# Ten gathered tiles instead of eight beside an attention, and one graph's product moved between the scoring matmuls

## The chip, the cores and the metric

The kernel runs on one core of one Trainium2 chip. The metric is the device time of one execution in microseconds (us), the median of several runs. A profile is one further execution, recorded instruction by instruction.

## The reference

Input x is 64 graphs of 256 nodes with 256 features; adj is one sparse symmetric 256x256 weight matrix, the same for every graph. Four layers follow each other: three "scoring" layers (L0, L1, L3) and an attention layer (L2) between the second and the third of them. Cut to what matters, with the batch index left out:

```
scoring layer:
  pre_u = h @ W1[:256];  pre_v = h @ W1[256:]
  S[u,v] = sigmoid(relu(pre_u[u] + pre_v[v] + b1) . W2 + b2)
  a = (S * adj)^T @ h                    # only pairs (u,v) with an edge matter
  m = (adj @ h) * h                      # called "mixed" in the kernel
  h = beta1*h + beta2*(a @ Wa + ba) + beta3*(m @ Wm + bm)
attention layer:
  f = h @ W1^T;  f1 = f . W2 + b2
  h = softmax(leaky_relu(f1[i] + f1[j]) + adj) @ f + bias2 + h
```

## The kernel before, in words

**Tiling.** Since S is multiplied by adj, a score is needed only for node pairs with an edge. The kernel numbers the edges on the chip (`edges`, once) and sorts them into 16 blocks of up to 128 pairs, each given by a triple (k, m, i); the diagonal (`own`) and up to 64 pairs that don't fit (`left`) are kept apart. One block of two graphs is a tile of 128 pairs x (2 graphs x 256 features). Its sum pre_u[u] + pre_v[v] is made in one of two ways:

- The eight blocks in FAST are *made* on the tensor engine: ScalarE copies rows of pu and pv into `pre` (`rows_u`, `rows_v`, lines 754 and 763), and a matmul with the 0/1 matrix `pick` (L700) puts the 128x512 sums into PSUM pool `ga`, which has three buffers.
- The eight blocks in FETCHED are *fetched*: pu and pv are written to tables in DRAM (L633, SP queue), and the GpSimd queue issues two indirect DMAs per tile (L745, `fetch`): one gathers the rows of u, the second gathers those of v and adds them. The list FETCHES sets their order, 18 issues a stage with the two for `left`; `issue_after` keeps them in that order. The first six (AHEAD) are issued as soon as the first half of the tables is written, the others when the stage begins that scores this pair.

Either way VectorE then does two operations per tile (`rated`, L664), one a graph: relu, times w2row, summed into a column of `raw`. ScalarE turns columns into scores by a tanh (`rated_all`, L684): first the EARLY columns (the blocks with m = 0, the diagonal and `left`), then the LATE ones (m = 1). From these VectorE makes `rm` (L692).

**Staging.** Graphs are taken in pairs, in two streams "a" and "b" of 16 pairs each. While one pair is being scored (the *heavy* side: `scores`, with its iterators `made`, `got` and `end`), the other goes through everything else (the *light* side): `after` (`spread` puts the scores back into `sa`, L790 and L792; `finish` makes the layer's output, L281 with `sa`, L369 or L355), the attention, and `before` (the products with W1, L628, copies to pu and pv, L629 and L630, the table writes, and at its end `mixed`, L281 with `adj`). One such pairing is a stage, one call of `beside`. Six stages make a round, and there are 16 rounds, 96 stages:

| stage | scored (heavy) | beside it (light) |
|---|---|---|
| 1 | a, L0 | b: after L3, before L0 of the next pair |
| 2 | b, L0 | a: after L0, before L1 |
| 3 | a, L1 | b: after L0, before L1 |
| 4 | b, L1 | a: after L1, attention, before L3 |
| 5 | a, L3 | b: after L1, attention, before L3 |
| 6 | b, L3 | a: after L3, before L0 of the next pair |

So `mixed` of the pair that stage 4 scores is done at the end of stage 3, and that of stage 5 at the end of stage 4. In what follows a stage is taken to begin at the LATE tanh of the stage before.

**What sets the order.** Each engine runs its own queue in the order in which a scheduler put it when the program was built. The source steers it by hand: every `yield` of the light side says how many tiles of `made` and of `got` are to be placed there (`yield 0, 1`: none made, one fetched), and `beside` advances both iterators by that. `early` (L774 and L778: the `left` pairs and the diagonal go into `sa`) follows the sixth fetched tile. At the end of `before` stands `yield REST_OF_IT`, which places all tiles that are left, and then comes `mixed`, whose matmuls run on the tensor engine while the last scores, their tanh and `rm` are made. The multiplication of `mixed` by hT on VectorE (L795) is kept back in the list `later` until `spread` has been done.

**Buffers.** The first four fetched tiles (FIRST) have a buffer for each stream; the other four share one buffer. PSUM has five buffers `ps` and three `ga`.

Of the kernel before, what the change touches and what calls it, by code (L numbers as in the profile page):

```python
# [9 lines left out]
FP = mybir.dt.float32  # L10
# [5 lines left out]
P = 128  # L16
# [16 lines left out]
FAST = [(0, 0, 2), (0, 0, 3)] + [(0, 1, i) for i in range(4)] + [(1, 0, 2), (1, 0, 3)]  # L33
FETCHED = [(k, 0, i) for k in range(2) for i in (0, 1)] + [(1, 1, i) for i in range(4)]
FIRST = 4

FETCHES = [(0, 0), (1, 0), (2, 0), (0, 1), (3, 0), (1, 1)]
FETCHES += [(-1, 0), (2, 1), (4, 0), (3, 1), (5, 0), (-1, 1), (6, 0), (4, 1), (7, 0), (5, 1), (6, 1), (7, 1)]

AHEAD = 6  # L40

# [16 lines left out]
def quarter(q):  # L58
    return slice(q * 64, (q + 1) * 64)

# [18 lines left out]
def adj_seq_kernel(ctx: ExitStack, tc: tile.TileContext, a: dict, out: bass.AP):  # L79
# [15 lines left out]
    mm = nc.tensor.matmul  # L95
# [36 lines left out]
    def z_weights(l):  # L132
        for kept, n, beta in ((wm, "Wm", "beta3"), (wa, "Wa", "beta2")):
            kept[l] = const.tile([P, 2, D], FP, name=l + n)
            nc.sync.dma_start(out=kept[l], in_=a[l + n].rearrange("(c p) e -> p c e", p=P))
            nc.scalar.mul(kept[l], kept[l], sca(l + beta))
        zbias[l] = const.tile([P, 2], FP, name=l + "zbias")
        zb = const.tile([P, 2], FP, name=l + "zb")
        nc.vector.tensor_scalar(zb, vecs[:, VEC[l + "ba"], :], sca(l + "beta2"), None, ALU.mult)
        nc.vector.scalar_tensor_tensor(  # L140
# [5 lines left out]
    for l in GNN:  # L146
        halfb2[l] = const.tile([P, 1], FP, name=l + "halfb2")
        nc.vector.tensor_scalar(halfb2[l], sca(l + "b2"), 0.5, None, ALU.mult)
    twob2 = const.tile([P, 1], FP, name="twob2")
    nc.vector.tensor_scalar(twob2, sca("L2_gnn_b2"), 2.0, None, ALU.mult)  # L150
# [7 lines left out]
    def counts(keep, pool, pc):  # L158
# [3 lines left out]
        nc.vector.tensor_scalar(mask, adj, 0.0, None, ALU.not_equal)  # L162
# [6 lines left out]
        nc.vector.tensor_tensor_scan(upto.rearrange("p s v -> p (s v)"), flat, flat, 0.0, ALU.add, ALU.bypass)  # L169
        past = pool.tile([P, 8], FP, name="past")  # L170
        nc.vector.memset(past, 0.0)
        nc.vector.tensor_copy(past[:, 1:8], upto[:, 0:7, 63])
        deg = pool.tile([P, 8], FP, name="deg")
        nc.vector.tensor_tensor(deg, upto[:, :, 63], past, ALU.subtract)
# [17 lines left out]
        nc.vector.tensor_copy(first, t[:, 0:8])  # L192
        last = keep.tile([P, 8], FP, name="last")
        nc.vector.tensor_tensor(last, first, deg, ALU.add)

        over = pool.tile([P, 8], FP, name="over")
        nc.vector.tensor_scalar(over, t[:, 8:16], -128.0, 0.0, ALU.add, ALU.max)
        begin = keep.tile([P, 9], FP, name="begin")
        nc.vector.memset(begin, 0.0)
        nc.vector.tensor_tensor_scan(begin[:, 1:9], over, over, 0.0, ALU.add, ALU.bypass)  # L200
        t = pc()
        mm(out=t[:, 0:1], lhsT=other, rhs=begin[:, 8:9], start=True, stop=True)
        nc.vector.tensor_scalar(begin, begin, t[:, 0:1], None, ALU.add)
        number = keep.tile([P, 8, 64], FP, name="number")
        shift = pool.tile([P, 8], FP, name="shift")
        nc.vector.tensor_tensor(shift, first, past, ALU.subtract)
        nc.vector.tensor_tensor(number, upto, shift.unsqueeze(2).to_broadcast([P, 8, 64]), ALU.add)
        nc.vector.tensor_tensor(number, number, mask.rearrange("p m (s v) -> p (m s) v", v=64), ALU.mult)
# [3 lines left out]
    with tc.tile_pool(name="pc", bufs=2, space=bass.MemoryType.PSUM) as pc, tc.tile_pool(name="cnt", bufs=1) as cnt:  # L212
# [3 lines left out]
        nc.vector.tensor_scalar(many, end, float(LEFT), None, ALU.is_gt)  # L216
# [11 lines left out]
    def attention_weights(one, psum):  # L228
# [8 lines left out]
        nc.vector.tensor_copy(w2q[:, :, D], t[:, 0:2])  # L237
        for c in range(2):
            nc.vector.tensor_scalar(qb[:, c, :], ones, w2q[:, c, D : D + 1], None, ALU.mult)

    def last_bias(one):
# [3 lines left out]
        nc.vector.tensor_scalar(zbrow, zbrow, sca(LAST + "beta2"), None, ALU.mult)  # L245
        nc.vector.scalar_tensor_tensor(zbrow, bmrow, sca(LAST + "beta3"), zbrow, ALU.mult, ALU.add)
# [19 lines left out]
    def stages(pools):  # L266
# [16 lines left out]
        def flip(o, src):  # L283

            for m in range(2):
                for c in range(2):
                    nc.tensor.transpose(o[:, m, blk(c)], src[:, c, blk(m)], ident)  # L287
# [22 lines left out]
        def mixed(st, l, later=None):  # L310

            st["mT"] = mT = one.tile([P, 2, 2, N], FP, tag="mT" + st["side"], name="mT")
            for g in range(2):
                t = psum()
                product(t, st["h"][g], adj)
                times = (mT[:, :, g, :], t, st["hT"][:, :, g, :], ALU.mult)
                if later is None:
                    nc.vector.tensor_tensor(*times)
# [647 lines left out]
```

## Time and profile before

| what | value |
|---|---|
| median of 3 runs | 3519.05 us (3515.6 to 3520.39) |
| the profiled execution's own time | 3512.57 us |
| its span, first to last instruction | 3510.1 us |
| granted TensorE clock | 0.993 |
| busy: PE matmul / PE weight load | 3447.8 us (98%) / 2108.7 us (60%) |
| busy: VectorE / ScalarE / GpSimd | 2610.0 us (74%) / 1598.8 us (46%) / 2230.7 us (64%) |
| DMA: moved, mean rate | 587.25 MB, 167 GB/s |
| queue 0 (the fetches): bytes, share of 16 engines | 427.93 MB, 61.4% |

The page lists PE (matmul), PEld (weight load, overlaps PE), DVE (VectorE), ACT (ScalarE), POOL (GpSimd) and SP (the queue that issues plain DMAs). A row of a timeline has the start in us, the time from the first start to the last end, engine, line, operation, out<-in, the shape, and how many instructions were merged; in brackets the idle time of the engine before it and what ended it. Ends of matmuls are modelled and consecutive matmuls overlap, so the distance between starts tells more than a length. A product of fp32 operands shows as two matmul records, so one made tile is two L700 records (1536 in 96 stages of eight tiles).

Over stages 2 to 95 of the trace, measured from LATE tanh to LATE tanh, the medians of the six stages are 31.1, 32.6, 32.3, 40.0, 42.6 and 35.2 us.

### The profile page before, as it was taken

Reading aid. Unit: us, or ns where it says so; the run is one execution under the profiler, and the core shown is the slowest. Engines: PE = TensorE matmul, PEld = TensorE weight load, DVE = VectorE, ACT = ScalarE, POOL = GpSimd, SP = SyncE. Lnnn points to the kernel's source line nnn. Section 1 sums busy time; section 2 is a strip of 40 time slices with the busy share of each in tenths; the row PEclk is TensorE's granted clock in tenths of the full one; section 3 lists DMA queues with packets and bytes.
Section 4 is the critical chain, followed back from the end, with each engine's and each line's share of the span. In section 5 each row is a group of like instructions: output and inputs, shape, how many; then the busy total and the mean of one; then the engine's idle time right before and its main releaser. Section 6 shows DMA issues by size and latency. Waiting matters only on the chain.

```text
span 3510.1 us, 48385 instructions
## 1 busy us (share of the span) xinstructions
PE 3447.8 (98%) x14328; PEld 2108.7 (60%) x14328; DVE 2610.0 (74%) x10584; ACT 1598.8 (46%) x2929; POOL 2230.7 (64%) x1754
## 2 busy tenths in 40 slices
PE   6999999999999999999999999999999999999998
PEld 3566565656656566565666656656565665656655
DVE  5778686777777777777777777768677777777776
ACT  2454444444444444544444444444444444445452
POOL 3757667575666757667576675766757566675764
PEclk7999999999999999999999999999999999999999
DMA  5768777686777868778687786877768687786865
GB/s 149 168 151 189 155 184 165 163 180 153 186 156 174 177 143 193 158 175 182 142 195 158 181 170 155 188 155 185 163 165 178 149 188 154 179 181 148 192 148 114
DMA packets 274733, 587.25 MB, mean 167 GB/s; under 512 B 37024, under 2 KB 54304, under 8 KB 274464
## 3 DMA queue, kind: packets, MB, share of 16 engines
q0 software_dynamic: 190464, 427.93, 61.4%
q1 hardware_dynamic: 82416, 154.96, 12.6%
q8 instruction: 116, 1.90, 0.2%
q10 hardware_dynamic: 1584, 1.20, 0.1%
q14 instruction: 153, 1.25, 0.1%
HBM read 466.51 MB, written 117.44 MB: 166 GB/s over the span
## 4 chain that ended last, share of the span: by engine, by line
PE 67%; DVE 4%; POOL 3%; DMA 3%; issue 2%; ACT 0%; POOLq 0%; DVEq 0%
PE ps L281 13%; PE ga L700 13%; PE ps L628 12%; PE ps L369 8%; PE ps L355 5%; PE ps L790 4%; PE ps L451 3%; PE ps L410 3%; POOL fetched L745 2%; PE ps L287 2%; DMA fetched<-tablev,ids_v 2%; PE ps L774 2%; DVE junk L664 2%; PE ps L404 1%; DVE rm L692 1%
## 5 line engine op out<-in xcount | busy, mean ns | idle before, releaser
L745 POOL DMA_INDIRECT fetched<-tablev,ids_v x768 | 1211.3, 1577 | 351.0 <-issue 237.4
L745 POOL DMA_INDIRECT fetched<-tableu,ids_u x768 | 766.8, 998 | 806.1 <-DMA tableu<-pu 576.1
L700 PE MATMUL ga<-pre,pick 128*128 128x512 f32 x1536 | 775.2, 604 | 10.5 <-DVE junk L664 7.9
L628 PE MATMUL ps<-L_gnn_w,hT 128*128 128x512 f32 x1536 | 695.4, 596 | 5.7 <-DMA hT<-in_xT_dram 5.7
L664 DVE SCALAR_TENSOR_TENSOR junk<-ga,L_gnn_w2row 128x256 f32<-128x256 f32 x1536 | 583.5, 420 | 119.8 <-PE ga L700 114.8
L664 DVE SCALAR_TENSOR_TENSOR junk<-fetched,L_gnn_w2row 128x256 f32<-128x256 f32 x1536 | 596.1, 419 | 32.6 <-DMA fetched<-tablev,ids_v 32.1
L763 ACT COPY pre<-pv 64x512 f32<-64x512 f32 x768 | 473.4, 616 | 107.1 <-DVE pv L630 76.3
L628 PEld LDWEIGHTS ps<-L_gnn_w,hT 128*128 128x128 f32 x1536 | 285.1, 191 | 334.6 <-issue 311.2
L754 ACT COPY pre<-pu 64x1024 f32<-64x1024 f32 x384 | 392.9, 1039 | 3.8
L700 PEld LDWEIGHTS ga<-pre,pick 128*128 128x128 f32 x1536 | 274.9, 191 | 163.6 <-issue 111.9
L372 DVE TENSOR_TENSOR hT<-hb,ps 128x512 f32<-128x512 f32 x128 | 88.0, 688 | 379.0 <-PE ps L369 379.0
L281 PE MATMUL ps<-adj,h 128*128 128x256 f32 x1536 | 361.0, 387 | 6.6 <-DVE own L639 4.7
L281 PE MATMUL ps<-sa,h 128*128 128x256 f32 x1536 | 363.7, 382 | 3.0 <-DVE sa L792 2.6
L281 PEld LDWEIGHTS ps<-sa,h 128*128 128x128 f32 x1536 | 288.9, 190 | 119.3 <-issue 47.3
L629 ACT COPY pu<-ps 128x256 f32<-128x256 f32 x384 | 142.2, 370 | 467.6 <-PE ps L628 449.1
L281 PEld LDWEIGHTS ps<-adj,h 128*128 128x128 f32 x1536 | 284.0, 190 | 77.0 <-issue 34.3
L692 DVE TENSOR_TENSOR rm<-gva,val 128x256 f32<-128x256 f32 x768 | 277.4, 420 | 37.9 <-ACT val L685 27.7
L333 ACT ACTIVATE hb<-hT,L_gnn_zbias,scas 128x512 f32<-128x512 f32 x128 | 97.4, 807 | 450.4 <-DVE hT L372 363.7
L790 PEld LDWEIGHTS ps<-rm,gu 128*64 128x64 f32 x3072 | 175.0, 137 | 123.1 <-PE ps L281 59.1
L369 PE MATMUL ps<-mT,L_gnn_Wm 128*128 128x512 f32 x512 | 240.6, 592 | 0.0
L369 PE MATMUL ps<-aT,L_gnn_Wa 128*128 128x512 f32 x512 | 240.6, 592 | 0.0
L790 PE MATMUL ps<-rm,gu 128*64 128x128 f32 x3072 | 218.5, 280 | 14.6 <-DVE rm L692 12.4
(156 smaller groups left out, 4074.3 us busy)
## 6 DMA issues: line engine op xcount, KB each, us to landing
tableu<-pu SPq DMA_DIRECT2D x192, 256.0 KB
tablev<-pv SPq DMA_DIRECT2D x192, 256.0 KB
hT<-in_xT_dram SPq DMA_DIRECT2D x32, 512.0 KB
h<-in_x_dram SPq DMA_DIRECT2D x64, 256.0 KB
out_dram<-h SPq DMA_DIRECT2D x64, 256.0 KB
fetched<-tableu,ids_u POOLq DMA_INDIRECT x768
fetched<-tablev,ids_v POOLq DMA_INDIRECT x768
L_gnn_w<-in_L_gnn_W_dram SPq DMA_DIRECT2D x6, 256.0 KB
```

What stands on the lines that cost most here:

```text
L281: mm(out=o[:, m, :], lhsT=lhs[:, c, blk(m)], rhs=rhs[:, c, :], start=c == 0, stop=c == 1)
L355: mm(out=z[:, m, :], lhsT=y[:, c, g, blk(m)], rhs=w[:, c, :], start=j == 0 and c == 0, stop=j == 1 and c == 1)
L369: mm(out=z, lhsT=w[:, c, blk(m)], rhs=y[:, c], start=j == 0 and c == 0, stop=j == 1 and c == 1)
L628: mm(out=t, lhsT=hT[:, c, g, blk(m)], rhs=w1[l][:, c], start=c == 0, stop=c == 1)
L629: nc.scalar.copy(pu[:, m, g, :], t[:, 0, :])
L664: nc.vector.scalar_tensor_tensor(junk, t, 0.0, w2row[l], ALU.max, ALU.mult, accum_out=raw[:, i : i + 1])
L692: nc.vector.tensor_tensor(rm[:, k, ms, g, :], gva[:, k, ms, :], val[:, i : i + 4].unsqueeze(2).to_broadcast([P, 4, 64]), ALU.mult)
L700: mm(out=t, lhsT=pick[:, k, 4 * m + i, :], rhs=pre[:, n], start=True, stop=True)
L745: this = nc.gpsimd.indirect_dma_start(out=to, out_offset=None, in_=rows, in_offset=bass.IndirectOffsetOnAxis(ap=ids, axis=0), compute_op=( ...
L754: nc.scalar.copy(st["pre"][h, f : f + n], st["pu"][h, m].rearrange("p g d -> p (g d)").unsqueeze(1).to_broadcast([64, n, 2 * D]),)
L763: nc.scalar.copy(st["pre"][halves[1 - k], n], st["pv"][halves[i % 2], i // 2].rearrange("p g d -> p (g d)"))
L790: mm(out=t[h, :, quarter(i)], lhsT=gu[:, k, 4 * m + i, :], rhs=rm[:, k, 4 * m + i], start=True, stop=True)
```

## The change

- **Beside an attention** (stages 4 and 5; `more` names the pairs: b at L1, a at L3) the last two tiles of FAST, (0,1,2) and (0,1,3), are fetched too: ten fetched, six made. Their four indirect DMAs stand among the last of FETCHES_MORE, 22 issues instead of 18. The shared buffer of the later fetched tiles grows from four to six tiles.
- **Half of mixed as a filling.** In these two stages `before` does `mixed` for graph 0 only; graph 1's four products are put into `made` behind its third tile, write to a `ga` buffer, and are multiplied by hT at once.
- **Order of tiles.** FAST now begins with the four blocks of m = 0, so the EARLY tanh needs four made tiles rather than all, and the placing lists are new (STEPS for `finish`, `beside` in `before`).
- **Where the light side is "after L0, before L1"** (stages 2 and 3, `placed`), the made tiles, the fetched tiles' scores, the diagonal's and the tanh are tied behind the last instruction issued on their engine (`behind`, with a recording wrapper `Noting` around the engines), and `early` comes before the fifth fetched tile.
- **The diagonal of L1** is made from pu and pv in SBUF by one 128x512 addition per half, in `scores`, rather than by two 128x256 additions that read PSUM in `before`.

Through `Noting`, nearly every compute instruction of the changed kernel is recorded under one line of that wrapper, L79. The core of the diff:

```diff
-FAST = [(0, 0, 2), (0, 0, 3)] + [(0, 1, i) for i in range(4)] + [(1, 0, 2), (1, 0, 3)]
+FAST = [(k, 0, i) for k in range(2) for i in (2, 3)] + [(0, 1, i) for i in range(4)]
+MORE = FAST[6:]
-FETCHES += [(-1, 0), (2, 1), (4, 0), (3, 1), (5, 0), (-1, 1), (6, 0), (4, 1), (7, 0), (5, 1), (6, 1), (7, 1)]
+FETCHES += [(-1, 0), (2, 1), (4, 0), (3, 1), (-1, 1), (5, 0), (6, 0), (4, 1), (7, 0), (5, 1), (6, 1), (7, 1)]
+FETCHES_MORE = FETCHES[:-2] + [(8, 0), (6, 1), (9, 0), (7, 1), (8, 1), (9, 1)]
+STEPS = {
+    GNN[0]: [(1, 1), (1, 1), (0, 1), (1, 0), (0, 1), (2, 1)],
+    GNN[1]: [0, 0, 0, (0, 1), (0, 1), 1],
+    LAST: [1, 1, (0, 1), (1, 1), (0, 1), (2, 1)],
+}
...
-        def mixed(st, l, later=None):
+        def mixed(st, l, later=None, graphs=(0, 1), buffers=None):
...
+                t = buffers.tile([P, 2, 256], FP, tag="ga", name="ga") if buffers else psum()
...
+        def more(st, l):
+            return (st["side"], l) in (("a", LAST), ("b", GNN[1]))
...
-            got = {LAST: (1, 0, 1, 1), GNN[1]: (1, 1, 1, 1), GNN[0]: (0, 0, 2, 1)}[l]
+            beside = {LAST: [0, (0, 1), (0, 1), (0, 1)], GNN[1]: [0] + [(0, 1)] * 3, GNN[0]: [0, 0, (0, 2), (0, 1)]}[l]
...
-            yield from mixed(st, l, later if past else None)
+            yield from mixed(st, l, later if past else None, (0,) if more(st, l) else (0, 1))
...
+            blocks, fast = (FETCHED + MORE, FAST[:6]) if more(st, l) else (FETCHED, FAST)
+            t = one.tile([P, len(FETCHED + MORE) - FIRST, 2, D], FP, tag="fetched", name="fetched")
...
             def made():
-                for n, (k, m, i) in enumerate(FAST):
+                for n, (k, m, i) in enumerate(fast):
                     t = ga.tile([P, 2, D], FP, tag="ga", name="ga")
-                    mm(out=t, lhsT=pick[:, k, 4 * m + i, :], rhs=pre[:, n], start=True, stop=True)
+                    with stay(tensor):
+                        mm(out=t, lhsT=pick[:, k, 4 * m + i, :], rhs=pre[:, n], start=True, stop=True)
...
+                    if n == 2 and more(st, l):
+                        yield from mixed(st, l, None, (1,), ga)
...
-                        for _ in made:
-                            yield
-                        rated(left, REST)
+                        if placed:
+                            while len(count) < 4:
+                                next(made)
+                        else:
+                            for _ in made:
+                                yield
+                        with stay(vector):
+                            rated(left, REST)
                         rated_all(EARLY, 0)
                         yield
+                        if placed:
+                            early(st)
+                            yield
...
-                    if f == FIRST + 1:
+                    if f == FIRST + 1 and not placed:
                         early(st)
```

The order that the build gives the tensor engine between `early` of one stage and of the next, counted in matmuls of the program (two records each), shows the move. Stage 4 into 5, the part up to the first products with the scores, and the part within the attention:

```
before                                  changed
ro,guo x4  adj,h x8  pre,pick x1        ro,guo x4  gnn_w,hT x4  adj,h x4
rm,gu x16  pre,pick x1                  rm,gu x8  pre,pick x1  rm,gu x8  pre,pick x1
sa,h x8                                 sa,h x8
...
w2q,hT x8  pre,pick x3  ident,e x4      w2q,hT x8  adj,h x4 (into ga)  pre,pick x1  ident,e x4
```

## The prediction

> **What bounds the kernel now.** I read the page first: its engine shares and the group of the made tiles.
>
> ```profile
> span 3510.1 us, 48385 instructions
> PE 3447.8 (98%) x14328; PEld 2108.7 (60%) x14328; DVE 2610.0 (74%) x10584; ACT 1598.8 (46%) x2929; POOL 2230.7 (64%) x1754
> L700 PE MATMUL ga<-pre,pick 128*128 128x512 f32 x1536 | 775.2, 604 | 10.5 <-DVE junk L664 7.9
> ```
>
> PE has work from end to end. Busy alone proves little, since matmuls overlap, so I took the distances between their starts. Within a run of like records they are 0.429 us for 512 columns and 0.216 for 256. Summed at these prices, a stage of the middle rounds leaves only 0.9 to 2.1 us, 9.1 us a round of 213. Some 7.4 of that repeats at fixed places, where matmuls of other row or column groups follow each other (0.1 to 0.2 us each). True waits are about 1.7 us a round: 0.5 before stage 2 (`mixed` waits for PSUM that VectorE's `own` holds), 0.8 before stage 3 and 0.4 before stage 4 (L790 waits for `rm`). So PE's issue is the bound in each stage; taking a matmul away pays as long as nothing else comes late.
>
> Next the timeline of PE where stage 4 ends and 5 begins (tanh at 1915.77), and in the attention of stage 5:
>
> ```profile
> 1909.01 5.32 PE L628 MATMUL ps<-L_gnn_w,hT 128*128 128x512 f32 x12
> 1914.25 1.13 PE L774 MATMUL ps<-ro,guo 64*128 64x256 f32 x8
> 1915.32 3.72 PE L281 MATMUL ps<-adj,h 128*128 128x256 f32 x16
> 1918.88 1.02 PE L700 MATMUL ga<-pre,pick 128*128 128x512 f32 x2
> 1919.83 1.97 PE L790 MATMUL ps<-rm,gu 128*64 128x128 f32 x32
> 1921.72 1.12 PE L700 MATMUL ga<-pre,pick 128*128 128x512 f32 x2
> ...
> 1939.97 2.74 PE L700 MATMUL ga<-pre,pick 128*128 128x512 f32 x6
> 1942.54 0.60 PE L287 MATMUL ps<-ident,e 128*128 128x128 f32 x4
> ```
>
> No row has an idle bracket. Between the last product with W1 and L790, PE has 5.6 us of cover (1914.25 to 1919.83) for scores, tanh and `rm`; inside the attention three made tiles (2.57 us) cover the softmax.
>
> Then ScalarE and VectorE over the same boundary, which give what that cover hides:
>
> ```profile
> 1913.05 1.04 ACT L754 COPY pre<-pu 64x1024 f32<-64x1024 f32 x1
> 1914.10 1.24 ACT L763 COPY pre<-pv 64x512 f32<-64x512 f32 x2
> 1915.37 0.37 ACT L629 COPY pu<-ps 128x256 f32<-128x256 f32 x1
> ```
>
> ```profile
> 1916.84 1.25 DVE L778 SCALAR_TENSOR_TENSOR sa<-diag,val,ps 128x256 f32<-128x256 f32 x3
> 1918.01 1.42 DVE L692 TENSOR_TENSOR rm<-gva,val 128x256 f32<-128x256 f32 x4
> ```
>
> `rm` is done at 1919.43, 0.4 us before PE asks, and 1.6 us of its lateness is `early` (L778), queued ahead of it. Last the GpSimd queue, stage 5's chain of fetches:
>
> ```profile
> 1915.31 0.98 POOL L745 DMA_INDIRECT fetched<-tableu,ids_u  x1 [15.29 <-DMA tableu<-pu]
> ...
> 1919.96 1.56 POOL L745 DMA_INDIRECT fetched<-tablev,ids_v  x1 [1.16 <-DMA fetched<-tableu,ids_u]
> 1921.83 0.98 POOL L745 DMA_INDIRECT fetched<-tableu,ids_u  x1 [0.31 <-issue]
> ...
> 1942.82 1.54 POOL L745 DMA_INDIRECT fetched<-tablev,ids_v  x1 [0.30 <-issue]
> 1957.87 0.98 POOL L745 DMA_INDIRECT fetched<-tableu,ids_u  x1 [13.50 <-DMA tableu<-pu]
> ```
>
> Eighteen issues take 29 us, then GpSimd idles 13.5 us until the next tables are written. An issue costs 0.98+0.30 us (u) or 1.55+0.30 (v). The first v waits for the first u to land, 4.65 us after its issue; the trace's DMA records put the last packet of stage 5's chain 4.3 to 5.7 us (median 5.2) after the last issue began.
>
> **What the Trainium skill says.** "Perfetto Trace Analysis", Identifying the Most-Contended Engine: matmul busy time is no good measure of how near PE is to its peak. The trace agrees: the made tile's record lasts 604 ns, its starts are 429 apart; I price by starts. "TensorE: Matmul & The Clock Gate", Back-to-back issue gap: about N/2.4 + 2.5 ns, 216 for 512 columns. Here the gap is 429, twice that for each record, and a tile has two; the measured value is used. "DMA: Bandwidth & Descriptors", Anatomy of one DMA — SWDGE (gpsimd) path: about 2.0 us plus bytes/436e3, an estimate of 2.6 us for a fetch of 256 KB. The trace shows 4.65 and 5.2 with other fetches in flight; I take 5.2. "Perfetto Trace Analysis", DMA Instruction — SWDGE (GPSIMD): the profiled window is the writing of descriptors, not the movement, which fits a 1.55 us row that lands 5 us after its start.
>
> **The change, part by part.**
>
> *Two tiles less to make.* Four records of 0.429 us are 1.72 us of PE a stage; 32 stages: **-54.9 us**. With them go one L754 copy and two of L763 (2.3 us of ScalarE a stage, which at 46% gains nothing). VectorE's scoring is the same for both kinds, 419 and 420 ns: zero.
>
> *Two tiles more to fetch.* 2 x (1.28 + 1.85) = 6.3 us of GpSimd and 1 MB of DMA a stage. It lies in the idle 13.5 us (15.3 in stage 4), which shrink to 7, if the last tile lands in time. In stage 5 the chain starts, by the new order, about 5.6 us after the second product with W1 (4.6 before; the third now stands behind `early`'s matmuls). The last v is issued 33.7 us into the chain, so it lands at 5.6 + 33.7 + 5.2 = 44.5 us. The next stage's same point comes 40.8 us after (42.6 less 1.72), and VectorE asks for the tile 4.0 us past that (1.0 matmuls of `early`, 1.7 L778, 0.7 another tile, the rest pv): 44.8. Spare 0.3 us, and about 1.6 more before PE notices at L790, since `mixed` after stage 5 is whole. I take zero; the ends are -0 and +1.5 us in stage 5 (+24). Stage 4's chain starts 4.4 us before its stage, so it has some 4 us more room. Queue 0 rises from 4.46 to 5.5 MB in these stages, whose DMA share is 0.63 and 0.69 now: no limit. The first two fetched tiles are now scored inside `finish`, about 12 us into stage 5, when the second has just landed (v issued at 7.3, plus 5.2); VectorE idles some 4 us there before hT (L372), so a short wait costs nothing, one over 4 us would hold hT.
>
> *Half of mixed moved.* Its eight records (1.72 us) are neither added nor removed. In the attention they stand in for the two tiles that went: 1.72 + 0.86 = 2.58 us of filler against 2.57, so the softmax stays covered. Its multiplication by hT (0.68 us, L795 before) is queued on VectorE ahead of the second graph's maxima (L423) and holds one of three `ga` buffers meanwhile; two tiles' scores (1.4 us) that stood ahead of them are gone: nothing. At the boundaries into stages 4 and 5 they are missed, but `early` has moved ahead of the last products too. Into stage 5, from the end of `early`'s matmuls: PE 3.5 (two products with W1) + 1.7 (half of mixed) + 1.0 (first half of L790) + 1.05 (a made tile) = 7.3; VectorE and ScalarE: the ScalarE queue above (pre, pre, pu) delays the last pu to 5.0, pv 5.35, tanh and add 5.5, `rm` and one `own` 7.4, plus 0.2 to reach PE. Wait: 0.3 us. Into stage 4 the same sum gives 8.2 for PE and 9.3 + 0.2 for `rm` less one made tile, 9.15: 0.35, against 0.4 now. A `rm` that is wholly uncovered would cost 1.72 in both; a gain isn't excluded (0.4). I take +0.25 a round. The order also puts a made tile between the halves of L790 in these two stages (0.15 + 0.10 + 0.09 + 0.10 us of switching in the rows before stage 1) and takes one away before stage 2: net +0.44.
>
> *Stages 2 and 3.* `early` comes before the turn (L287) and the last products, so L778 no longer stands ahead of `rm`: from the end of its matmuls `rm` is ready at 8.8, and PE asks for its second half at about 9.8. The 0.8 before stage 3 goes. `own` of L1 no longer reads PSUM, so the 0.5 before stage 2 goes: **-1.3 us a round**. The ends are 0 (a new wait takes their place) and -1.3. Ties add no wait between engines; behind a tied instruction that waits stand the later tiles' scores and pv, for which PE has several us of other work. Bounds: -0.3 to +1 us a stage, taken zero. The L1 diagonal costs 0.69 instead of 0.84 us of VectorE a half: nothing.
>
> Sum a round: -3.43 - 1.3 + 0.25 + 0.44 = -4.0 us; over 16 rounds -65, less about a tenth for the edges, where the first rounds' waits are others: **-58 us**. The profiled execution, 3512.6 us (3510.1 of span and 2.5 around), would become 3454; it lies 6.5 us below the median, 3519.05, which becomes **3461**.
>
> **The rivals.**
> - *The cover is missed (20%).* `rm` comes later than my sum and the waits of stages 4 and 5 grow by 0.5 to 1.5 us each: 16 to 48 us back, 3477 to 3509. For it: the spare times are tenths of a us, and the outcome hangs on ScalarE's queue. Against: L778 left the way.
> - *The last fetch decides, slower (6%).* If the ninth and tenth tile land late in both attention stages, LATE tanh, `rm` and L790 wait, and each us costs 32 us. It turns slower from 1.8 us in both stages beyond what is covered; at 2.5 us the time is 3461 + 80 = 3541. For it: stage 5's spare of 0.3. Against: stage 4's spare, the 7 us that GpSimd still idles, and DMA shares well under those of stage 6 (0.89).
> - *The tiles were free fillings (3%).* If they only filled waits, removing them changes nothing: 3519. Against: no idle brackets, and the same amount of filler in the new order.
>
> **How the numbers follow.** The likeliest case, PE stays the bound (68%), covers 3440 to 3477; better than that 3%. What a measurement can tell from no change is 0.2%, 7 us. Range 3442 to 3495: it holds most of the first case and the larger part of the first rival. Faster 0.91, same 0.03, slower 0.06.
>
> **What would show it.** Made-tile records fall from 1536 to 1408, fetches rise by 128. Stages 4 and 5 become 1 to 2 us shorter, 2 and 3 about 0.5, 1 and 6 stay. GpSimd's wait for tables falls by some 200 us in all. Wrong it would be if L790's wait for `rm` grows in stages 4 and 5, if VectorE's wait for fetched tiles (32 us now) grows, or if stages 2 and 3 get longer.

## The result and the profile after

| | before | changed |
|---|---|---|
| median | 3519.72 us (3515.6 to 3520.84) | 3497.7 us (3493.48 to 3503.58) |
| ratio, with its 95% interval | | 0.9942 [0.9926, 0.9958] |
| profiled execution, and its span | 3512.57, 3510.1 us | 3499.89, 3498.2 us |
| granted clock | 0.993 | 0.993 |

The change gains 22 us. The forecast was 58 us, and 3497.7 lies just outside its range (3442 to 3495). In the two profiled executions the spans differ by 11.9 us only: that of before lies 7 us under its median, that of the changed kernel 2 us above. The page of the changed kernel, the parts that answer to those shown of before:

```profile
span 3498.2 us, 48226 instructions
PE 3391.1 (97%) x14200; PEld 2079.5 (59%) x14200; DVE 2626.2 (75%) x10526; ACT 1554.0 (44%) x2833; POOL 2409.6 (69%) x1882
...
q0 software_dynamic: 204800, 461.49, 66.6%
...
L79 PE MATMUL ga<-pre,pick 128*128 128x512 f32 x1408 | 721.5, 607 | 36.0 <-ACT pre L79 24.6
```

The counts are those of the forecast: 1408 records of made tiles for 1536, 128 issues more on GpSimd. What is new stands at the end of the last line: TensorE idled 36 us ahead of made tiles, 24.6 of them for `pre`, ScalarE's copy. Before it was 10.5, most of it for VectorE. The waits of TensorE in the whole trace (us in total, times, the longest one), first of the kernel before, then of the changed one:

```profile
PE ps L790 <- DVE rm L692: 12.4, 10, 6.0
PE ga L700 <- DVE junk L664: 7.9, 3, 6.8
...
PE ps L281 <- DVE own L639: 4.7, 5, 2.4
```

```profile
PE ps L79 <- DVE rm L79: 31.0, 33, 6.0
PE ga L79 <- ACT pre L79: 24.6, 30, 1.3
```

Summed over all its rows this view gives 57.5 us of waiting before and 102.1 after: 44.6 more. The work that went is 54.9 us by the prices of the forecast, and 54.9 less 44.6 is 10.3, near the 11.9 by which the spans differ. So the sum fits tiles that were worth what was forecast, with waits that took most of it back: 18.6 us more for `rm` and 24.6 for `pre`, for which the view of before has one wait of 0.3 us. A second pair of traces, c_before and c_after of the third series below, gives the same sum: 59.8 and 97.4 us of waits, 37.6 more, and spans that differ by 15.7 us.

From LATE tanh to LATE tanh the medians of the six stages, measured as for before, are now 31.1, 30.9, 32.5, 40.6, 42.4 and 35.1 us. Stages 4 and 5, which lost the tiles, were to become 1 to 2 us shorter; stage 4 is 0.6 longer and stage 5 only 0.1 shorter. Only stage 2 gained clearly, 1.6 us. (The half of `mixed` that moved also carries TensorE work from stage 3 to 4 and from 4 to 5, so the sum says more than one stage.)

*Where `pre` is late.* The boundary from stage 4 into stage 5 (LATE tanh at 1904.58), TensorE first, then ScalarE:

```profile
1898.37 1.13 PE L79 MATMUL ps<-ro,guo 64*128 64x256 f32 x8
1899.44 3.70 PE L79 MATMUL ps<-L_gnn_w,hT 128*128 128x512 f32 x8
1902.97 1.89 PE L79 MATMUL ps<-adj,h 128*128 128x256 f32 x8
1904.80 1.09 PE L79 MATMUL ps<-rm,gu 128*64 128x128 f32 x16
1906.90 1.12 PE L79 MATMUL ga<-pre,pick 128*128 128x512 f32 x2 [1.01 <-ACT pre L79]
```

```profile
1902.92 1.24 ACT L79 COPY pre<-pv 64x512 f32<-64x512 f32 x2
1904.19 0.37 ACT L79 COPY pu<-ps 128x256 f32<-128x256 f32 x1
1904.58 0.31 ACT L79 ACTIVATE val<-raw,L_gnn_halfb 128x16 f32<-128x16 f32 x1
1904.93 0.22 ACT L79 ACTIVATE val<-val 128x16 f32<-128x16 f32 x1
1905.17 1.04 ACT L79 COPY pre<-pu 64x1024 f32<-64x1024 f32 x1
1906.23 2.53 ACT L79 COPY pre<-pv 64x512 f32<-64x512 f32 x4
```

The made tile at 1906.90 is the new stage's first. Its last row copy is the first of the four at 1906.23 (2.53/4 = 0.63 us, so done at 1906.86). Ahead of it on ScalarE stand the copy of the last product (pu), tanh, the addition and the 1.04 us copy for tiles 2 and 3. From the start of half of `mixed` (1902.97, the last product just ended) to `pre` that is 3.9 us; TensorE has 1.83 + 1.09 us of work for it, 2.9. Before, ScalarE's queue began in the same way (last pu, tanh, addition, a 1.04 us copy, then `pre`), but between the last product and the first made tile lay `early`'s matmuls and the whole of `mixed`: 1914.25 to 1918.88, 4.6 us. At the boundary into stage 6 `mixed` is whole, and only `early` has moved away ahead of the products:

```profile
1940.64 1.13 PE L79 MATMUL ps<-ro,guo 64*128 64x256 f32 x8
1941.71 3.70 PE L79 MATMUL ps<-L_gnn_w,hT 128*128 128x512 f32 x8
1945.24 3.62 PE L79 MATMUL ps<-adj,h 128*128 128x256 f32 x16
1949.59 1.12 PE L79 MATMUL ga<-pre,pick 128*128 128x512 f32 x2 [0.72 <-ACT pre L79]
```

Over the whole trace the wait into stage 5 is there in all 16 rounds, 16.4 us in sum, and that into stage 6 in 13 of them, 7.4 us.

*Where `rm` is late.* At the start of stage 2 the second half of L790 now follows the first without a made tile between; it waits in 13 of the 16 rounds, 10.1 us in sum (0.43 us in most, 1.1 to 2.1 in four), more than the 4.7 us of the PSUM wait (`own`) that went there. At the start of stage 4 it waits 7.9 us in 11 rounds and at the start of stage 1 4.5 us in six. Each of these, and three of the four long ones at the start of stage 2, begins 2.6 to 2.9 us after a wait of VectorE for a fetched tile, and is as long as that to within about half a us (in round 11 at the start of stage 1, 1.22 us for 1.25); the plain 0.43 us of stage 2 has none ahead of it. The 5.7 us at the start of stage 3 went. VectorE's waits show the late tiles, first of the kernel before, then of the changed one:

```profile
DVE hT L372 <- PE ps L369: 379.0, 128, 4.6
...
DVE junk L664 <- DMA fetched<-tablev,ids_v: 32.1, 25, 2.9
```

```profile
DVE junk L79 <- DMA fetched<-tablev,ids_v: 203.7, 148, 3.1
...
DVE hT L79 <- PE ps L79: 100.4, 75, 2.7
```

The wait for fetched tiles rose from 32.1 to 203.7 us. Most of it (3.7 and 5.4 us a stage) is in stages 4 and 5, nearly all at the first two fetched tiles, where VectorE had waited for TensorE anyway: its waits for L369's PSUM (hT) fell from 379 to 100 us. In the last 8 us before a LATE tanh, where a late tile delays `rm`, it is 2.3 us a round in the 13 rounds of the middle, for 1.5 before.

### The profile page after: what moved, and what is told of

The parts are those of the page before. It is cut to its first block, busy times and chain, and to the rows that moved or that the text cites. A ratio compares the mean times of both kernels' runs of the same rounds, so it can differ in the third digit from the quotient of the medians.

```text
span 3498.2 us, 48226 instructions
## 1 busy us (share of the span) xinstructions
PE 3391.1 (97%) x14200; PEld 2079.5 (59%) x14200; DVE 2626.2 (75%) x10526; ACT 1554.0 (44%) x2833; POOL 2409.6 (69%) x1882
## 4 chain that ended last, share of the span: by engine, by line
PE 62%; POOL 10%; DMA 10%; DVE 8%; issue 7%; ACT 3%; another core or an unknown queue 0%; POOLq 0%; ACTq 0%; SPq 0%; DVEq 0%
PE ps L79 48%; PE ga L79 13%; POOL fetched L820 9%; DMA fetched<-tablev,ids_v 6%; DVE junk L79 3%; DMA fetched<-tableu,ids_u 3%; ACT pre L79 2%; DVE rm L79 1%; POOL left L820 1%; DVE sa L79 1%; DMA tableu<-pu 1%; DVE own L79 1%; ACT val L79 1%; ACT pu L79 1%; DVE mT L79 0%
## 5 line engine op out<-in xcount | busy, mean ns | idle before, releaser
L820 POOL DMA_INDIRECT fetched<-tablev,ids_v x832 | 1313.7, 1579 | 415.3 <-issue 256.1
L820 POOL DMA_INDIRECT fetched<-tableu,ids_u x832 | 840.5, 1010 | 548.8 <-DMA tableu<-pu 285.4
L79 DVE SCALAR_TENSOR_TENSOR junk<-fetched,L_gnn_w2row 128x256 f32<-128x256 f32 x1664 | 642.4, 418 | 205.8 <-DMA fetched<-tablev,ids_v 203.7
L79 PE MATMUL ga<-pre,pick 128*128 128x512 f32 x1408 | 721.5, 607 | 36.0 <-ACT pre L79 24.6
L79 PE MATMUL ps<-L_gnn_w,hT 128*128 128x512 f32 x1536 | 706.7, 597 | 5.8 <-DMA hT<-in_xT_dram 5.8
L79 DVE SCALAR_TENSOR_TENSOR junk<-ga,L_gnn_w2row 128x256 f32<-128x256 f32 x1408 | 537.3, 419 | 110.6 <-PE ga L79 94.6
L79 PEld LDWEIGHTS ps<-L_gnn_w,hT 128*128 128x128 f32 x1536 | 279.7, 190 | 323.2 <-issue 296.3
L79 ACT COPY pre<-pv 64x512 f32<-64x512 f32 x704 | 434.1, 617 | 70.8 <-DVE pv L79 47.3
L79 ACT COPY pre<-pu 64x1024 f32<-64x1024 f32 x352 | 361.4, 1044 | 7.4
L79 PE MATMUL ps<-sa,h 128*128 128x256 f32 x1536 | 359.8, 380 | 4.7 <-DVE sa L79 4.7
L79 PEld LDWEIGHTS ps<-sa,h 128*128 128x128 f32 x1536 | 291.7, 190 | 114.4 <-issue 62.5
L79 PEld LDWEIGHTS ga<-pre,pick 128*128 128x128 f32 x1408 | 248.5, 190 | 183.6 <-issue 92.5
L79 ACT COPY pu<-ps 128x256 f32<-128x256 f32 x384 | 142.8, 372 | 478.2 <-PE ps L79 450.3
L79 ACT ACTIVATE hb<-hT,L_gnn_zbias,scas 128x512 f32<-128x512 f32 x128 | 97.4, 807 | 479.3 <-DVE hT L79 368.1
L79 DVE TENSOR_TENSOR rm<-gva,val 128x256 f32<-128x256 f32 x768 | 279.8, 419 | 28.7 <-ACT val L79 21.2
L79 PE MATMUL ps<-adj,h 128*128 128x256 f32 x1280 | 296.8, 383 | 3.9 <-issue 3.9
L79 PEld LDWEIGHTS ps<-adj,h 128*128 128x128 f32 x1280 | 241.6, 191 | 74.1 <-issue 40.0
L79 DVE TENSOR_TENSOR pv<-ps,L_gnn_b1row 128x256 f32<-128x256 f32 x384 | 161.3, 420 | 135.5 <-ACT pu L79 128.8
L79 PEld LDWEIGHTS ps<-rm,gu 128*64 128x64 f32 x3072 | 174.7, 137 | 144.5 <-issue 54.1
L79 PE MATMUL ps<-rm,gu 128*64 128x128 f32 x3072 | 218.8, 280 | 32.6 <-DVE rm L79 31.0
L79 ACT COPY aT<-ps 128x512 f32<-128x512 f32 x192 | 112.4, 585 | 299.7 <-PE ps L79 267.5
L79 PE MATMUL ps<-mT,L_gnn_Wm 128*128 128x512 f32 x512 | 240.6, 592 | 0.0
```

Source lines behind the costliest of these rows:

```text
L79: self.last = getattr(self.engine, op)(*a, **k)
L820: this = nc.gpsimd.indirect_dma_start(out=to, out_offset=None, in_=rows, in_offset=bass.IndirectOffsetOnAxis(ap=ids, axis=0), compute_op=( ...
```

## The experiments

Two theories were to be told apart. *A:* TensorE's new waits at the starts of stages 5 and 6 are the loss; cover was moved away, and the first made tile's copy is late in ScalarE's queue. *B:* the fetches are late; VectorE, which takes its work in order, waits for a tile near a stage's end, and tanh and `rm` come late behind it. A third possibility, that the placing and the ties as such cost time, is what undoing the two named parts leaves over.

The experiments ran in four series, each on one chip with its own runs of the kernel before (medians 3520.6, 3502.6, 3514.7 and 3515.3 us); the changed kernel was run again in the last two. Compare times within a series, and ratios to before across them.

### First series: parts undone, and ScalarE's order

x_first:

```diff
                     rows_v(st, 4 - 4 * m, 2, 0)
+                    st["first"] = scalar.last.ins
...
-                        with tc.issue_after(past[-1]) if past else nullcontext():
+                        with tc.issue_after(past[-1]) if past else nullcontext(), tc.issue_after(st["first"]):
```

> The changed kernel, but at the starts of stages 5 and 6 ScalarE copies the pre rows of made tiles 0 and 1 (pre<-pv, two copies) ahead of the pre<-pu copy of tiles 2 and 3, which takes 1.04 us. Nothing else moves. Theory A, the first made tile of the stage comes late because its own copy stands behind tanh, add and that long copy: TensorE's waits of 1.24 us (start of stage 5) and 0.74 us (start of stage 6) nearly go, 1.5 to 2.0 us a round, so 3466 to 3475 us. Theory B, late fetches hold VectorE and through it tanh and rm: the two waits stay or turn into waits for rm, and the time stays within 7 us of 3498.

x_whole:

```diff
-            yield from mixed(st, l, later if past else None, (0,) if more(st, l) else (0, 1))
+            yield from mixed(st, l, later if past else None)
...
-                    if n == 2 and more(st, l):
-                        yield from mixed(st, l, None, (1,), ga)
```

> The changed kernel with mixed whole at the end of before again: four products (1.72 us) return to the boundaries into stages 4 and 5, none of them is a filling in the attention; ten tiles stay fetched. Theory A: the wait of 1.24 us at the start of stage 5 goes and so does the 0.45 us at the start of stage 4, which gives 20 to 27 us; against it the softmax loses 1.72 us of filling in both stages, at most 55 us back and, as the wait for the logits of 0.17 us shows little, perhaps half of that: 3480 to 3510, with stage 5's wait moved from its start into the attention. The start of stage 6 keeps its 0.74 us. Theory B: the start of stage 5 keeps most of its wait, and the time rises to 3510 or more.

x_eight:

```diff
-                        st["fetches"] = list(FETCHES_MORE if more(st, l) else FETCHES)
+                        st["fetches"] = list(FETCHES)
...
-            blocks, fast = (FETCHED + MORE, FAST[:6]) if more(st, l) else (FETCHED, FAST)
+            blocks, fast = FETCHED, FAST
```

> The changed kernel with eight tiles fetched and eight made in every stage; half of mixed stays a filling. Two made tiles (1.72 us of TensorE) return to stages 4 and 5: 55 us. Theory A, the fetches cost nothing and the waits at the starts of stages 5 and 6 are ScalarE's order: they stay, and the time is 3545 to 3555. Theory B, the two additional fetches cost most of what is missing (about 36 us): the waits at the starts of stages 5 and 6 go, and the time is 3510 to 3525.

x_rest has x_whole's edit and x_eight's.

> The changed kernel with eight tiles fetched and mixed whole everywhere: what is left of the change is the order of FAST, the new placing lists, the ties in stages 2 and 3, early's place and the diagonal of L1. The prediction's working gives it -1.3 us a round for stages 2 and 3 and nothing else: 3499 us. Theory A: the wait at the start of stage 6 (0.74 us, 12 us in all) is there already, since it comes of the order, but not that of stage 5: 3505 to 3515. Theory B: neither is there, 3495 to 3502. If the placing itself is the cause, above 3519.

| kernel | median us | ratio to before |
|---|---|---|
| x_first | 3495.61 | 0.9934 [0.9913, 0.9956] |
| x_whole | 3567.32 | 1.0141 [1.0113, 1.0170] |
| x_eight | 3530.87 | 1.0033 [1.0020, 1.0047] |
| x_rest | 3554.80 | 1.0094 [1.0073, 1.0115] |

x_first fell where theory B had it, within 7 us of 3498. x_whole passed B's open line (3510 or more) by 57 us; x_eight lies between the two theories, and x_rest far above 3519, the line for the third possibility, that the placing itself costs time. The last three, with the changed kernel, make a two-by-two table, which teaches most. The new order alone (x_rest) is *slower* than before, by 34 us, where the forecast had put it at -1.3 us a round. (The new placing lists were made for six made tiles and half of `mixed` in stages 4 and 5, so x_whole, x_eight and x_rest also run with lists that weren't made for them.) With half of `mixed` as filling (x_eight) it is 10 us slower than before. The two tiles that are fetched gain about 33 us on top of that (3530.9 to 3497.7; by ratios 0.9%), not 55, and without the filling they *cost* some 12 us (x_rest to x_whole; the two intervals touch). The waits of TensorE go far to say why, of x_whole and then of x_rest:

```profile
PE ps L79 <- ACT logits L79: 42.1, 55, 1.0
PE ga L79 <- ACT pre L79: 26.3, 15, 2.4
```

```profile
PE ps L79 <- DVE sa L79: 32.0, 25, 2.8
PE ps L79 <- DVE rm L79: 21.6, 21, 5.6
```

In x_whole the softmax has no filling left in its second half and TensorE waits for the logits, 0.7 to 1.0 us at one or two places a stage. So the forecast's "the softmax stays covered" came true, but only because of this filling. In x_rest 22 of the 32 us for `sa` lie in stage 5 (5.3 us in x_eight); why `sa` comes late there was not followed up. Over all rows x_rest's waits are 105.2 us and x_whole's 157.3. Both traces also have eight short stretches at half the granted clock, 27 us in all (see the last section), an estimate of up to 14 us that the waits don't count.

x_first moved ScalarE's copies as planned. (In stage 5 the build also put the first made tile behind 6 of L790's records instead of 16, so not quite "nothing else" moved.) The waits for `pre` fell to 6.4 us, but the median moved by 2 us, less than its interval. So theory A in its plain form had failed: waits went, time did not.

### Second series: the last fetches, and early's place

x_landed:

```diff
-                    tile_scores(fetched[f], *block)
+                    tile_scores(fetched[f if f < 8 else f - 8], *block)
```

> The changed kernel, but the scores of the ninth and tenth fetched tile are computed from the first two tiles' buffers, which landed long before, so the result isn't the reference's; all 22 fetches are still issued and moved. Theory A, the lost gain is the first made tile's copy behind ScalarE's queue: nothing changes, 3490 to 3503. Theory B, the last two fetches land late and hold VectorE, then tanh and rm: VectorE's waits at the ends of stages 4 and 5 go, and 10 to 30 us come back, 3468 to 3488.

x_first_landed has this edit and x_first's.

> As x_landed (the ninth and tenth tile's scores are computed from the first two tiles' buffers, so the result isn't the reference's), with the ScalarE order of x_first. There the waits at the starts of stages 5 and 6 fell by 1.3 us a round in the trace, 22 us in all, but the time by hardly anything. Theory A with B behind it, what the start gives back is lost again to late fetches: 3465 to 3480. Theory A alone: within 5 us of x_first, 3490 to 3500.

x_early:

```diff
-                    if f == FIRST + 1 and not placed:
+                    if f == FIRST + (3 if more(st, l) else 1) and not placed:
                         early(st)
```

> The changed kernel with early placed behind the eighth fetched tile instead of the sixth in stages 4 and 5, so that its four matmuls (1.1 us) stand behind the last product with W1 again, as before. The boundary into stage 6 gets 1.1 us of cover back; in that into stage 5 they take the place of the first half of L790, which goes behind the made tile. Theory A: the wait of 0.74 us at the start of stage 6 goes, that of 1.24 at stage 5 becomes about 1.0: 3481 to 3487. Against it: L778 stands ahead of rm again and makes rm late, 0.5 us in both stages: 3495 to 3500. Theory B: no change, 3493 to 3503.

x_early_first has x_early's edit and x_first's.

> x_early with x_first's ScalarE order. Theory A: both waits at the starts are gone but for about 0.4 us in stage 5; 1.6 us a round, 3470 to 3478. If late fetches take it back as they seem to in x_first: 3485 to 3495.

| kernel | median us | ratio to before (3502.6 here) |
|---|---|---|
| x_landed | 3487.46 | 0.9954 [0.9940, 0.9968] |
| x_first_landed | 3481.96 | 0.9937 [0.9924, 0.9951] |
| x_early | 3469.62 | 0.9905 [0.9891, 0.9918] |
| x_early_first | 3466.37 | 0.9897 [0.9882, 0.9912] |

x_landed's 3487 lies in theory B's range only because everything ran faster in this series, the kernel before by 12 to 18 us. By the ratio the ninth and tenth tile cost nothing (0.9954 against 0.9942), and x_first_landed is where x_first was (0.9937 and 0.9934). The changed kernel itself was not run here, so a gain of some 10 us isn't excluded; 20 is. What helped was `early` back behind the last products: by the ratio 13 us, what theory A expected of it. Two things come with it, and no run tells them apart. The start of stage 6 has its 4.6 us of cover again, and the last two products, with them the tables and so the fetches, no longer stand behind 1.1 us of `early`'s matmuls. L778, which now stands ahead of `rm` again, cost nothing that can be seen. x_first's order on top (x_early_first) gives less than the intervals can tell. x_early's TensorE waits are 14.3 us for `rm` and 13.8 for `pre`, for 31.0 and 24.6.

### Third series: the correction beside the changed kernel

c_before and c_after are the two kernels unchanged, c_early_first is x_early_first.

> The kernel before, once more and with a profile, beside the next three on one chip: the time before was 3520.6 us in one series and 3502.6 in the next. If that is the chip, the profile shows where 18 us lie: as waits of TensorE (clock and nominal time the same), or in the granted clock. Ratio to before 1.0.

> The changed kernel, once more, on the same chip as the other three, to compare the corrected order with it directly. Its waits at the starts of stages 5 and 6 are set by engines, not by transfers, so they stay at 1.2 and 0.7 us; ratio to before 0.993 to 0.996.

> x_early_first once more, beside the changed kernel. Theory A, the waits at the starts of stages 5 and 6 are what the forecast missed: 1.9 us a round or more against the changed kernel, 25 to 40 us, ratio to before 0.984 to 0.988. If only part of it reaches the end, as the first ratio to before says: 10 to 20 us, 0.988 to 0.991.

x_between is x_early_first and, in spread:

```diff
+            between = (st["side"], l) == ("a", GNN[0])
...
                 it = vector.tensor_tensor(sa[:, m], sa[:, m], t, ALU.add)
+                if m == 0 and between:
+                    yield 1
...
-            yield 1 if l == GNN[1] else 2
+            yield 1 if l == GNN[1] or between else 2
```

> x_early_first with one made tile moved between the two halves of L790 in stage 2, where the second half waits 0.67 us for rm since the ties hold the tile behind it. If that wait was hidden gain: 0.67 less 0.35 for switching, 0.3 us a round, 5 us faster than x_early_first. If the switching costs as much: no difference that can be told.

| kernel | median us | ratio to before (3514.65) |
|---|---|---|
| c_before | 3514.66 | 0.9999 [0.9992, 1.0006] |
| c_after | 3493.03 | 0.9946 [0.9932, 0.9959] |
| c_early_first | 3470.18 | 0.9870 [0.9855, 0.9885] |
| x_between | 3458.76 | 0.9842 [0.9828, 0.9855] |

Two edits of order, with the compute instructions of every engine the same in number, give 23 us and another 11 us. The result is 56 us faster than before. That this is nearly the forecast's 58 is in part luck, as the working has other parts (below). c_early_first is x_early_first again, and their ratios are 0.9870 and 0.9897: across series a ratio tells nothing finer than some 10 us. c_before's waits, 59.8 us, don't show what made 18 us between the first two series.

The correction is seen in the traces too. From c_after to c_early_first TensorE's waits fall from 97.4 to 67.6 us, those for `pre` from 25.0 to 3.3, and the span by 27.1 us. The boundary into stage 5 in c_early_first, to be held against the one above:

```profile
1893.71 3.68 PE L79 MATMUL ps<-L_gnn_w,hT 128*128 128x512 f32 x8
1897.32 1.13 PE L79 MATMUL ps<-ro,guo 64*128 64x256 f32 x8
1898.38 1.99 PE L79 MATMUL ps<-adj,h 128*128 128x256 f32 x8
1900.73 1.12 PE L79 MATMUL ga<-pre,pick 128*128 128x512 f32 x2 [0.35 <-ACT pre L79]
1901.78 2.37 PE L79 MATMUL ps<-rm,gu 128*64 128x128 f32 x32
```

The wait for `pre` is 0.35 for 1.01 us here (8 of 16 rounds have one at all). Then the start of stage 2 in c_after and in x_between:

```profile
1801.53 1.09 PE L79 MATMUL ps<-rm,gu 128*64 128x128 f32 x16
1803.15 1.42 PE L79 MATMUL ps<-rm,gu 128*64 128x128 f32 x16 [0.53 <-DVE rm L79]
1804.51 1.98 PE L79 MATMUL ga<-pre,pick 128*128 128x512 f32 x4
```

```profile
1785.65 1.09 PE L79 MATMUL ps<-rm,gu 128*64 128x128 f32 x16
1786.67 1.13 PE L79 MATMUL ga<-pre,pick 128*128 128x512 f32 x2
1787.73 1.09 PE L79 MATMUL ps<-rm,gu 128*64 128x128 f32 x16
```

The made tile between the halves covers the rest of `rm`. In the changed kernel the ties keep it behind both. In c_early_first's trace this wait is there in 15 rounds and sums to 13.1 us; in x_between's it is gone, and 11 us of time with it, where 5 had been expected. TensorE's waits in the whole trace of x_between sum to 56.8 us, as much as before (57.5), and its span, 3457.1 us, is 53.0 below before's for 54.9 us of work less:

```profile
PE ps L79 <- DVE rm L79: 16.4, 17, 4.9
...
PE ga L79 <- ACT pre L79: 4.3, 9, 0.9
```

### Fourth series: how the loss splits

d_after is the changed kernel and d_first is x_first, now side by side. x_free is the changed kernel with:

```diff
-                        tile_scores(fetched[f], *block)
+                        tile_scores(fetched[f % FIRST], *block)
```

> The changed kernel on the same chip as the next three, ratio to before 0.993 to 0.996.

> x_first once more, beside the changed kernel on the same chip. If the waits at the starts of stages 5 and 6 count in full: 15 to 21 us less than it. If something else takes them back: 0 to 8 us less.

> The changed kernel, but the scores of the fetched tiles from the fifth on are computed from the first four tiles' buffers in every stage, so the result isn't the reference's; all fetches are still issued and moved. No score then waits for a late fetch but those of the first four tiles. If late fetches hold a good part of the 36 us: 20 us or more less than the changed kernel. If they hold little: 0 to 10 us less.

x_between_free is x_between with the same edit.

> x_between (early behind the eighth fetched tile in stages 4 and 5, x_first's ScalarE order, one made tile between the halves of L790 in stage 2), with the fetched tiles from the fifth on scored from the first four tiles' buffers as in x_free, so the result isn't the reference's. x_between took 3459 us. If the fetches have become the limit behind TensorE, 10 us or more are to be had still: under 3449. If not: 3452 to 3459.

| kernel | median us | ratio to before (3515.33) |
|---|---|---|
| d_after | 3494.58 | 0.9943 [0.9923, 0.9963] |
| d_first | 3492.65 | 0.9936 [0.9922, 0.9950] |
| x_free | 3480.08 | 0.9895 [0.9881, 0.9909] |
| x_between_free | 3459.56 | 0.9843 [0.9831, 0.9856] |

d_first repeats x_first: 2 us less than the changed kernel. TensorE's waits of d_after and then of d_first tell where the rest went:

```profile
PE ps L79 <- DVE rm L79: 30.2, 28, 5.6
PE ga L79 <- ACT pre L79: 23.8, 28, 2.1
```

```profile
PE ps L79 <- DVE rm L79: 41.8, 42, 5.2
...
PE ga L79 <- ACT pre L79: 6.0, 15, 0.4
```

The waits for `pre` fall by 17.8 us and those for `rm` rise by 11.6. The new ones lie where stage 6 ends: 14.9 us in 13 rounds, for 4.6 in six rounds of d_after; in x_first it is 12.0 in 12 rounds. One of them in d_first, VectorE, ScalarE (the LATE tanh) and TensorE:

```profile
1769.84 0.43 DVE L79 SCALAR_TENSOR_TENSOR junk<-fetched,L_gnn_w2row 128x256 f32<-128x256 f32 x1 [1.69 <-DMA fetched<-tablev,ids_v]
```

```profile
1770.65 0.31 ACT L79 ACTIVATE val<-raw,L_gnn_halfb 128x16 f32<-128x16 f32 x1 [4.49 <-DVE junk L79]
```

```profile
1772.42 1.42 PE L79 MATMUL ps<-rm,gu 128*64 128x128 f32 x16 [1.65 <-DVE rm L79]
```

The last tile comes late, and tanh and `rm` behind it. TensorE reaches that point earlier than in d_after, the tile doesn't: VectorE's waits for fetched tiles in the last 8 us of stage 6 go from 0.24 to 0.83 us a round. x_free points the same way. Its scores wait for none but the first four tiles, and 14.5 us of time come back; its trace has

```profile
PE ps L79 <- DVE rm L79: 9.4, 16, 3.0
```

So theory B has its part too. But it is not shown for the ninth and tenth tile, as the forecast's rival had it; stage 6, for one, fetches eight. In the changed order the last issue of a stage lies 7 to 8 us ahead of the LATE tanh in *every* stage (medians of 13 rounds of the middle: 7.7, 7.7, 7.1, 8.5, 7.1, 7.4); before it was 8.3, 10.0, 10.6, 17.4, 15.5 and 7.9. In stages 2 to 5 the last packet lands 5.3 to 5.9 us after the last issue began (medians; before 5.2 to 5.9), and two scores of 0.42 us follow, so by these figures the edge is an estimated 6 to 7 us.

x_between_free gains nothing over x_between of the third series (ratios 0.9843 and 0.9842). That does not prove that the fetches are harmless there: its trace has a new wait for `sa` in stage 5, 15.9 us in 13 rounds, while the waits for `rm` fall from 16.4 to 3.0. Why `sa` comes late is left open.

## Why the prediction was wrong, point by point

- *Two tiles less to make, -54.9 us:* right, as far as the sum of work and waits above can show. TensorE has 128 matmul records less (14328 to 14200), all of made tiles. VectorE's cost was unchanged (418 and 419 ns a score).
- *Half of mixed moved, +0.25 us a round:* this is the step that failed first; the boundaries that it and `early`'s move touch cost 24.6 us of waits for `pre` alone, some 1.5 us a round. The sum into stage 5 was right for `rm`: forecast to be ready 7.4 us after `early`'s matmuls, found at 7.5 (from 1899.44 to 1906.9). But it counted the stage's first made tile as 1.05 us of cover, and that tile hangs on the same ScalarE queue: its own copy was done 7.4 us after them too. Cover that itself waits for what it is to cover covers nothing. The forecast quoted the queue, but on ScalarE its sum ended with tanh and the addition, two rows ahead of that copy. It then took the boundary into stage 6 as untouched ("1 and 6 stay"), although it said itself that `early` has moved, and read that move only as L778 getting out of the way; it took 1.1 us of matmuls from behind the last product as well.
- *Two tiles more to fetch, zero:* wrong in size. x_free puts late fetches at 14.5 us in the changed kernel (what they cost before was not measured, and how much of it the two new tiles cause isn't shown). That stage 5 has hardly any spare was seen (0.3 us forecast). Its chain takes 35.8 us from the first issue to the last, for 33.7 forecast, and GpSimd idles 5.4 us behind it, for 7. What was missed is that the order moved the other chains towards the edge too: stage 4's starts 2.9 us ahead of its stage where the forecast had taken the 4.4 of before, and stage 3's 2.2 where it was 5.4. GpSimd's wait for the tables fell by 290 us, not 200.
- *Stages 2 and 3, -1.3 us a round:* half right. The waits for `own` and the 0.8 us before stage 3 went. At the start of stage 2 a wait for `rm` took their place, which the text had named as the lower end: 10.1 us in the trace. x_between, which takes it away, gained 11 us.
- *Switching, +0.44:* not told apart.
- *The rivals:* "the cover is missed" (3477 to 3509, 20%) names the number that came and the right queue, ScalarE's. Its mechanism came only in part: the wait into stage 5 is for `pre`, not `rm`, a second one is at stage 6, and late fetches have their share. Of the signs that the text named against itself, one showed plainly: VectorE's wait for fetched tiles grew from 32 to 204 us. The other, `rm` at stage 4, is weak: by the length of L790's rows it waited some 0.4 us a round before, and the view gives 0.5 after, with single waits up to 1.65.

The late waits hide one another, so their prices don't add: taking only `pre` away gave 2 us, only the late fetches 14.5, both corrections of order 34. That is 34 of the 36 us that were missing. It doesn't confirm every part of the sum: x_between's gain is 54.9 us of work and next to nothing in waits, while the forecast's 58 is 54.9 and 9.8 us from all its other parts together, less a tenth.

## What to carry to other kernels

When cover is moved, list everything that the engine behind it does until the *first* instruction that TensorE then needs, and check for each piece of cover whether it waits for the same queue. Do that at every boundary that the order touches, not only at those that the diff speaks of. And a wait that vanishes from a trace is no gain until the time says so: with a second chain (here the fetches) close behind, what one gives back the other can take.

## What was not expected of the hardware

Long waits of TensorE cost more than themselves. Between the first 110 and the last 80 us of the 18 traces the granted clock falls to half 32 times, mostly for a single stretch of 3.4 us (three times 6.8). Each time TensorE had waited 1.56 us or longer, and the stretch began between 1.6 us before that wait's end and 1.7 us after it. Of the 48 waits of 1.8 us and more 29 were followed by such a stretch, of the 20 between 1.5 and 1.6 three, of the 16 between them none, and none of the 897 shorter ones by itself. One of d_after, with the clock (the third figure from the end) and the made tile behind the wait, which takes 1.87 us to the next start for some 1.0 elsewhere:

```profile
802.52 1.75 PE L79 MATMUL ps<-rm,gu 128*64 128x128 f32 x16 [1.96 <-DVE rm L79]
804.20 2.08 PE L79 MATMUL ga<-pre,pick 128*128 128x512 f32 x2
806.07 3.93 PE L79 MATMUL ps<-sa,h 128*128 128x256 f32 x16
```

```profile
803.30:806.70 3.40, 3.40 (x14) 1.95 (x9) 3.01 (x11) 1.09 (x2) 2.79 (x3) 0.50 0.84 164
```

A stretch at half clock loses at most 1.7 us, an estimate from its length. There are none in the profiled executions of the changed kernel and of x_between, four in d_after and eight each in x_whole and x_rest; why some long waits are followed by one and others not isn't shown.

This is part of why executions of one kernel spread. The changed kernel ran from 3487.3 us at a granted clock of 0.993 to 3510.2 at 0.989 in the fourth series, while all runs of x_between_free stayed within 2.2 us (3459.05 to 3461.24) at 0.993. The clock doesn't explain the series: at 0.992 the kernel before had a median of 3519.3 us in the first and of 3503.0 in the second, so kernels of different series were not compared by their times alone.
